# The silu and its table in program order, and TensorE's side products held behind the scan that precedes them

## The chip, the cores and the metric

The kernel runs on one core of a Trainium2 chip. The metric is the device time of one execution in microseconds (us), the median of several runs; lower is better. One execution was also recorded by the hardware profiler, and all durations below come from that record.

## What is computed

A batch of 16 images, 192 channels of 32 x 32, goes through four residual layers. Layers 0, 1 and 3 hold a recurrence along the 1024 pixels of an image; layer 2 is a depthwise convolution. The reference of layer 3, which matters most here, is in essence:

```python
xz = einsum('bchw,cd->bdhw', x, W_in) + b_in           # x: group-normed image
x_in, z = xz[:, :384], xz[:, 384:]
xc = silu(depthwise_conv4x4(x_in))                      # 384 channels
xs = [xc by rows, xc by columns, both reversed]         # 4 directions k
dt, Bm, Cm = projections of xs[k]; dt = softplus(dt)
h = h * exp(dt * A) + (dt * u) * B                      # per pixel, 16 states
y = sum(h * C)                                          # per pixel
y = layernorm(sum of the 4 directions) * silu(z)
g_out = y @ W_out + b_out
l_out = relu(bn(depthwise_conv3x3(x))) @ pw
out = w0 * g_out + w1 * l_out + x                       # w: softmax router
```

Layer 1 is of the same kind with one direction, a 4-tap convolution, two layer norms and a gate `silu(z)`.

## The kernel before

Three blocks of code run one after the other: `layer0`, `layer12` (layers 1 and 2) and `layer3`. Layers 1 and 3 are built around the same scan.

**The scan.** `scan_run` (L864) goes through units of 512 pixels and in each through the 16 states; one pair of unit and state is a step. Layer 1 has 2 units an image, so 32 steps, layer 3 has 4 directions of 2 units, so 128 steps. The 384 channels lie in three blocks t of 128 partitions. In a step

- `decay` (L904) makes exp(dt * A) on ScalarE (tile `da`, one instruction for each t, an `Exp`), for the step after this one;
- `times_b` (L882) makes u * B on ScalarE (tile `xbt`, three instructions; a fourth quarter is made on TensorE through `diag`, which GpSimd makes in `diagonals`), two steps ahead, and starts the DMA of one row of C to all partitions (tile `cb`);
- `turn` (L911) transposes xbt to the channel layout on TensorE (tile `xb`, four products for each t), one step ahead;
- `scan` (L925) is VectorE's recurrence instruction (tile `h`, L933), one for each t;
- `times_c` (L935) multiplies h by C on GpSimd (L940), after copying the last column to `carry` (L939);
- `total` (L942) transposes and adds h into `y` on TensorE (twelve products), two steps later.

`da` has five buffers, `xb` three, `h` four, `xbt` two.

**The side work.** All else of layers 1, 2 and 3 is written as Python generators that `Side` (L201) advances between the parts of a step (`side.tick`), each between a start and an end step. In layer 3, for image b, these are `prep` for the next unit (`scan_prep`, L827: softplus as an `Exp` at L841 and an `Ln` at L842 for each t, then transposes), `columns` and `tail` for the image before, `front`, `local`, `z` and `xc` for the image after.

**The tail.** `layer3_tail` (L1567) runs at steps 8 to 36 of the next image. For each half of an image it loads z (tile `tmp`, one buffer, L1574), does a layer norm (a `Square` at L361, an `Ln` at L363, an `Exp` at L364), calls `self.silu(sz)` on the loaded z, scales (L1579), multiplies on GpSimd (L1583), and later projects (L1591).

**What sets the order.** The text gives a program; a scheduler then places each engine's instructions, and may move one ahead of or behind others of its engine where no data forbids it. Every engine executes its own list in the order placed. Two things bind the scheduler by hand: `tc.keep_in_program_order(...)` on an instruction, and `tc.add_manual_dep` with class `NoSync`, which orders two instructions and adds no semaphore. In `scan_run`, `in_order` (L874) chains the transposes and totals of the scan to one another in this second way; TensorE's other products ("side products") are not bound to the chain.

**Activation tables.** ScalarE's functions lie in table sets. `Silu` needs one set, `Exp` and `Ln` are together in the set called `natural_log_exp_and_others` (`LNEXP` in the text). A load (ACT_TABLE_LOAD in the profile, LoadActFuncSet in the built program) puts a set in place. The text asks for one only in `silu` (L1204), which runs the activation and then preloads `LNEXP`; only the preload is kept in program order. Any other load is put in where the placed order needs it, at the activation that needs it.

Of the kernel before, what the change touches and what calls it, by code (L numbers as in the profile page):

```python
# [19 lines left out]
HP = 96  # L20
# [212 lines left out]


class Chunk:

# [15 lines left out]
class Program:  # L252
    def __init__(self, tc, ins, out, at):
        self.tc, self.nc, self.ins, self.out = tc, tc.nc, ins, out
        self.at96, self.at128, self.atc, self.atc0 = at
        self.nb = ins["x"].shape[0]


# [62 lines left out]
    def group_norm(self, pool, psum, x):  # L321

        nc = self.nc
        st = pool.tile([HP, 2, 2, 6], F32, name="gnst")
        mv = pool.tile([HP, 2, 2], F32, name="gnmv")
        for m in range(2):
            for i, h in enumerate(halves()):
                nc.vector.bn_stats(st[:, m, i], x[:, m, h])
            nc.vector.bn_aggr(mv[:, m], st[:, m].rearrange("p a b -> p (a b)"))
            yield 1  # L330
        ps = psum.tile([128, 512], F32, name="mm")
        nc.tensor.matmul(ps[:HP, :2], self.k("group", HP), mv[:, :, 0], start=True, stop=True)
        mean = pool.tile([HP, 2], F32, name="gnmean")
        nc.vector.tensor_copy(mean, ps[:HP, :2])
        d = pool.tile([HP, 2], F32, name="gnd")
        nc.vector.tensor_tensor(d, mv[:, :, 0], mean, SUB)
        q = pool.tile([HP, 2], F32, name="gnq")
        nc.vector.tensor_tensor(q, d, d, MUL)
        nc.vector.tensor_tensor(q, q, mv[:, :, 1], ADD)
        yield 1  # L340
        ps = psum.tile([128, 512], F32, name="mm")
        nc.tensor.matmul(ps[:HP, :2], self.k("group", HP), q, start=True, stop=True)
        r = pool.tile([HP, 2], F32, name="gnr")
        nc.vector.tensor_scalar(r, ps[:HP, :2], EPS, None, ADD)
        self.pow_mhalf(r)
        yield 1
        return mean, r, d

    def layer_norm(self, pool, psum, xs, outs, ones, p, n):

        nc = self.nc
        mean = psum.tile([128, 512], F32, name="mm")
        for i, x in enumerate(xs):
            nc.tensor.matmul(mean[:p, :n], ones, x, start=i == 0, stop=i == len(xs) - 1)
        for x, o in zip(xs, outs):
            nc.vector.tensor_tensor(o, x, mean[:p, :n], SUB)
        yield len(xs)
        var = psum.tile([128, 512], F32, name="mm")
        for i, o in enumerate(outs):
            sq = pool.tile([128, 512], F32, name="lnsq", bufs=1)  # L360
            nc.scalar.activation(sq[:p, :n], o, AF.Square)  # L361
            nc.tensor.matmul(var[:p, :n], ones, sq[:p, :n], start=i == 0, stop=i == len(xs) - 1)
        nc.scalar.activation(var[:p, :n], var[:p, :n], AF.Ln, bias=self.k("eps", p))  # L363
        nc.scalar.activation(var[:p, :n], var[:p, :n], AF.Exp, scale=-0.5)  # L364
        for o in outs:
            nc.vector.tensor_tensor(o, o, var[:p, :n], MUL)
        yield len(xs)
# [433 lines left out]
    def scan_rows(self, seen, w_x, n, bp, dp, psum):  # L801

        nc = self.nc
        ident = self.k("ident")
        m = w_x[0].shape[1]
        ps = psum.tile([128, 512], F32, name="mm")
        for t in range(3):
            nc.tensor.matmul(ps[:m], w_x[t], seen[:, t], start=t == 0, stop=t == 2)  # L810
        dbl = bp.tile([m, 512], F32, name="dbl", bufs=n)
        nc.scalar.activation(dbl, ps[:m], AF.Identity, bias=self.k("ones_row", m))
        row = dp.tile([n, NS, 512], F32, name="row", bufs=5)
        for q in range(n):
            nc.sync.dma_start(row[q], dbl[64 * q + RK + NS : 64 * q + XD])
        yield 2.6
        ps = psum.tile([128, 4, 128], F32, name="mm")
        for c in range(4):
            nc.tensor.transpose(ps[:, c, :m], dbl[:, c * 128 : (c + 1) * 128], ident[:m, :m])
        bt = bp.tile([128, 4, n, NS], F32, name="bt", bufs=4)  # L820
        nc.vector.tensor_copy(
            bt, ps.rearrange("p c (q r) -> p c q r", r=64)[:, :, :n, RK : RK + NS]
        )
        yield 0.5
        return dbl, row, bt

    def scan_prep(self, u, rows, q, xc, xt, new, w_dt, bp, psum):  # L827
# [9 lines left out]
        for t in range(3):  # L837
            ps = psum.tile([128, 512], F32, name="mm")
            nc.tensor.matmul(ps, w_dt[:, t * 128 : (t + 1) * 128], dbl, start=True, stop=True)  # L839
            e = bp.tile([128, 512], F32, name="lnsq", bufs=1)  # L840
# [6 lines left out]
        for j in range(3):  # L847
            o = slice(j * 512, (j + 1) * 512)
            if new:
                rows = xc[:, :, 512 * u.half : 512 * u.half + 512]  # L850
                ps = psum.tile([128, 512], F32, name="mm")
                for i in range(4):
                    c, t = divmod(4 * j + i, 3)
                    nc.tensor.transpose(ps[:, i * 128 : (i + 1) * 128], rows[:, t, c * 128 : (c + 1) * 128], ident)
                nc.scalar.copy(xflat[:, o], ps)
            ps = psum.tile([128, 512], F32, name="mm")
            for i in range(4):
                c, t = divmod(4 * j + i, 3)
                nc.tensor.transpose(ps[:, i * 128 : (i + 1) * 128], u.dt[:, t, c * 128 : (c + 1) * 128], ident)
            nc.vector.tensor_tensor(flat[:, o], xflat[:, o], ps, MUL)  # L860
# [3 lines left out]
    def scan_run(self, units, side, bp, psum):  # L864
# [6 lines left out]
        xbt, xb, da, h = {}, {}, {}, {}  # L871
        last = []

        def in_order(ins):  # L874

            if last:
                self.tc.add_manual_dep(
                    ins.ins, last.pop(), mybir.DependencyInfo(mybir.DependencyClass.NoSync, mybir.DependencyReason.DATA)
                )
            last.append(ins.ins.name)  # L880

# [96 lines left out]
        for i in range(len(steps) - 2, len(steps)):  # L978
            for t in range(3):
                total(i, t)  # L980
        side.close()

    def untranspose(self, y, t, psum):

        ps = psum.tile([128, 512], F32, name="mm")
        for c in range(4):
            self.nc.tensor.transpose(
                ps[:, c * 128 : (c + 1) * 128], y[:, c, t * 128 : (t + 1) * 128], self.k("ident")
# [99 lines left out]
    def depthwise(self, ps, blocks, reps, side):  # L1088

        width = W + side - 1  # L1090
        for r in range(side):
            for g, rep in enumerate(reps):
                seen = rep[:, : (15 + side) * width].rearrange("p (a b) -> p a b", b=width)[:, r : r + 16, :W]
                self.nc.tensor.matmul(  # L1094
                    ps[32 * g : 32 * g + 32], blocks[:, g * side + r], seen,
# [4 lines left out]
    def fold_norm(self, wp, psum, w, m_tiles, bias_in, bias, wname, bname, name):  # L1100
# [5 lines left out]
        for i in range(m_tiles):  # L1106
            for m in range(2):
                nc.tensor.matmul(
                    ps[:p, i : i + 1], w[:, m, i * p : (i + 1) * p], self.v96(bname, m), start=m == 0, stop=m == 1
# [35 lines left out]
    def layer1_front(self, b, sp, bp, psum):  # L1145
# [26 lines left out]
        for t in range(3):  # L1172
            for h in halves():
                ps = psum.tile([128, 512], F32, name="mm")
                for m in range(2):
                    nc.tensor.matmul(
                        ps, self.w_in[:, m, t * 128 : (t + 1) * 128], xn[:, m, h], start=m == 0, stop=m == 1
# [7 lines left out]
    def layer1_conv(self, b, bp, psum):  # L1185
# [3 lines left out]
        for t in range(3):  # L1189
            for h in halves():  # L1190
# [3 lines left out]
                for g, rep in enumerate(reps):  # L1194
                    nc.tensor.matmul(
                        ps[32 * g : 32 * g + 32], self.t_conv[:, 4 * t + g], rep[:, :512],
# [7 lines left out]
    def silu(self, x):  # L1204

        self.nc.scalar.activation(x, x, AF.Silu)
        self.tc.keep_in_program_order(self.nc.scalar.preload_act_table_set(LNEXP))

    def layer1_gate(self, b, bp, psum):
# [6 lines left out]
        for t in range(3):  # L1216
            for h in halves():
                ps = psum.tile([128, 512], F32, name="mm")
                for m in range(2):
                    nc.tensor.matmul(  # L1220
                        ps, self.w_in[:, m, DI + t * 128 : DI + (t + 1) * 128], xn[:, m, h], start=m == 0, stop=m == 1
# [6 lines left out]
    def layer1_out(self, b, bp, psum):  # L1228
# [6 lines left out]
        for h in halves():  # L1235
            for m in range(2):
                ps = psum.tile([128, 512], F32, name="mm")
                for t in range(3):
                    nc.tensor.matmul(
                        ps[:HP], self.w_out[:, t, m * HP : (m + 1) * HP], sz[:, t, h], start=t == 0, stop=t == 2  # L1240
# [6 lines left out]
    def layer1_tail(self, b, sp, bp, dp, psum):  # L1247
# [3 lines left out]
        for h in halves():  # L1251
# [8 lines left out]
            for m in range(2):  # L1260
                ps.append(psum.tile([128, 512], F32, name="mm"))
                for k in range(2):
                    nc.tensor.matmul(
                        ps[m][:HP], self.w_proj[:, k, m * HP : (m + 1) * HP], x[:, k, h], start=k == 0, stop=k == 1
# [212 lines left out]
    def layer3_local(self, b, sp, bp, psum):  # L1477
# [10 lines left out]
        for i, h in enumerate(halves()):  # L1488
# [10 lines left out]
            for m in range(2):  # L1499
                ps = psum.tile([128, 512], F32, name="mm")  # L1500
                for k in range(2):
                    nc.tensor.matmul(  # L1502
                        ps[:HP], self.w_pw[:, k, m * HP : (m + 1) * HP], l[:, k], start=k == 0, stop=k == 1
# [6 lines left out]
    def layer3_z(self, b, bp, psum):  # L1510

        nc = self.nc
        for i in range(2):
            for t in range(3):
                ps = psum.tile([128, 512], F32, name="mm")
                for m in range(2):
                    nc.tensor.matmul(  # L1517
                        ps, self.w_in[:, m, DI + t * 128 : DI + (t + 1) * 128],
# [7 lines left out]
    def layer3_xc(self, b, bp, dp, psum):  # L1526
# [6 lines left out]
        def project(t):  # L1533
            for i in range(2):
                ps = psum.tile([128, 512], F32, name="mm")
                for m in range(2):
                    nc.tensor.matmul(
                        ps, self.w_in[:, m, t * 128 : (t + 1) * 128],
# [28 lines left out]
    def layer3_tail(self, b, bp, psum):  # L1567
# [17 lines left out]
        for m in range(2):  # L1585
            for h in halves():
# [3 lines left out]
                for t in range(3):  # L1590
                    nc.tensor.matmul(  # L1591
                        ps[:HP], self.w_out[:, t, m * HP : (m + 1) * HP], v[:, t, h], start=t == 0, stop=t == 2
# [5 lines left out]
    def router(self, sp, psum, d, r):  # L1598
# [5 lines left out]
        for m in range(2):  # L1604
            wide = sp.tile([HP, HP], F32, name="wide", bufs=1)
            nc.vector.tensor_copy(wide, xm[:, m : m + 1].to_broadcast([HP, HP]))
            nc.tensor.matmul(ps[:HP, :2], wide, self.v96("3r_w", 2 * m, 2), start=m == 0, stop=m == 1)
        e = sp.tile([HP, 2], F32, name="re")
# [25 lines left out]
```

## Time and profile before

| | us |
|---|---|
| median of three runs | 17937.86 (17929.37 to 17949.53) |
| the profiled execution | 17942.07 |
| its span on the core | 17940.3 |
| PE busy | 16197.5 (90%) |
| DVE busy | 13314.9 (74%) |
| ACT busy | 12215.5 (68%) |
| POOL busy | 11472.7 (64%) |
| layer 1 and 2's scan, us 4310 to 7880: PE / DVE / ACT / POOL busy of 3570 | 3220.93 / 2729.63 / 2467.09 / 2092.00 |
| layer 3's scan, us 8112 to 17880: PE / DVE / ACT / POOL busy of 9768 | 8991.05 / 8490.39 / 8533.28 / 7894.56 |

PE is TensorE, DVE VectorE, ACT ScalarE, POOL GpSimd, SP the engine that issues most DMAs. The profiled execution is 4.2 us above the median. Its span is cut into layers by the records of the scan instruction (L933): the first one of layer 1 starts at 4310.6 us, the first one of layer 3 at 8112.7, and the last one ends at 17879.1. In layer 3 four engines are each busy for 81 to 92% of the time, so none of the busy shares alone says what sets the pace; the pace is read stretch by stretch.

A line of the groups reads: line, engine, operation, output<-inputs, shapes, count | busy us, mean ns of one | idle time of the engine just before them, and what ended it. A line of the stretches reads: the stretch, its length, then for each engine its busy time and number of instructions, the TensorE clock granted (1 is full), the DMA share and GB/s.

### The profile page before, as it was taken

The numbers are of one execution on the slowest core, as the hardware profiler recorded it, in microseconds if no ns is written. First come the engines' busy times: TensorE is split into PE (matmuls) and PEld (weight loads), VectorE is DVE, ScalarE is ACT, GpSimd is POOL, SyncE is SP. The second block draws the span as 40 slices with busy tenths as digits, with TensorE's granted clock in tenths as the row PEclk, the third lists the DMA queues.
The fourth block names the chain that finished last, engine by engine and source line by source line (L and its number), as shares of the span: only waits on it lengthen the run. The fifth ranks groups of instructions, "written<-read, shape, count | busy, mean of one in ns | idle before, by whom it ended". The sixth has DMA issues, their size and how long they took to land.

```text
span 17940.3 us, 264092 instructions
## 1 busy us (share of the span) xinstructions
PE 16197.5 (90%) x99836; PEld 11281.1 (63%) x99836; DVE 13314.9 (74%) x14875; ACT 12215.5 (68%) x19906; POOL 11472.7 (64%) x5556
## 2 busy tenths in 40 slices
PE   8999889898999999979899999999988999999998
PEld 4444444444655555546777777777777777777777
DVE  4444445444777777758888888888888888888888
ACT  2222222223766666647888898888888888988888
POOL 3333333333555555547787888787878877887878
PEclk8898898888999999989999999999999999999999
DMA  1111111112433333333333233333333332333232
GB/s 43 31 32 32 32 32 30 30 31 82 116 115 116 112 117 114 111 107 100 89 101 103 84 97 105 97 90 95 107 91 93 99 105 85 92 105 101 88 93 65
DMA packets 877953, 1511.12 MB, mean 84 GB/s; under 512 B 80336, under 2 KB 311197, under 8 KB 865834
## 3 DMA queue, kind: packets, MB, share of 16 engines
q1 hardware_dynamic: 876682, 1494.22, 28.6%
q8 instruction: 791, 12.96, 0.3%
q14 instruction: 480, 3.93, 0.1%
HBM read 1264.99 MB, written 228.92 MB: 83 GB/s over the span
## 4 chain that ended last, share of the span: by engine, by line
PE 27%; ACT 11%; DVE 8%; issue 4%; POOL 4%; DMA 1%; SPq 0%; POOLq 0%; DVEq 0%; ACTq 0%
PE y L951 7%; PE xb L917 6%; DVE h L933 6%; PE xb L920 4%; ACT da L909 4%; ACT xbt L889 3%; POOL h L940 3%; PE mm L1094 3%; PE mm L810 1%; PE mm L839 1%; PE mm L1517 1%; ACT L909 1%; ACT L842 1%; PE mm L1502 1%; ACT lnsq L842 1%
## 5 line engine op out<-in xcount | busy, mean ns | idle before, releaser
L940 POOL TENSOR_TENSOR h<-h,cb 128x1536 f32<-128x1536 f32 x2560 | 8880.1, 3472 | 1635.0 <-DVE h L933 1045.2
L909 ACT ACTIVATE da<-dt,neg_a 128x512 f32<-128x512 f32 x7680 | 5242.3, 714 | 1542.7 <-DVE h L933 1455.8
L933 DVE TENSOR_TENSOR_SCAN h<-da,carry,xb 128x512 f32<-128x512 f32 x3840 | 4664.9, 1262 | 812.8 <-PE xb L920 605.4
L951 PE MATMUL y<-const,h 128*128 128x128 f32 x30720 | 4739.7, 277 | 132.9 <-DVE ysum L1391 54.6
L933 DVE TENSOR_TENSOR_SCAN h<-da,xb 128x512 f32<-128x512 f32 x3840 | 4439.2, 1202 | 389.9 <-PE xb L920 255.2
L917 PE MATMUL xb<-const,xbt 128*128 128x128 f32 x23040 | 4128.4, 283 | 490.1 <-ACT xbt L889 266.7
L889 ACT ACTIVATE xbt<-ut,bt 128x384 f32<-128x384 f32 x7680 | 4172.9, 603 | 227.5 <-PE xb L917 225.0
L917 PEld LDWEIGHTS xb<-const,xbt 128*128 128x128 f32 x23040 | 2776.7, 143 | 1940.3 <-ACT xbt L889 678.8
L951 PEld LDWEIGHTS y<-const,h 128*128 128x128 f32 x30720 | 3705.2, 144 | 322.9 <-issue 258.8
L920 PE MATMUL xb<-diag,ut 128*128 128x128 f32 x15360 | 3028.5, 279 | 0.0
L920 PEld LDWEIGHTS xb<-diag,ut 128*128 128x128 f32 x15360 | 2400.0, 197 | 68.2 <-issue 68.2
L458 PE MATMUL conv<-ypad,w_conv 96*96 96x512 f32 x2304 | 1253.8, 665 | 3.1 <-ACT y L465 3.1
L899 POOL TENSOR_TENSOR diag<-const,bt 128x512 f32<-128x512 f32 x640 | 668.3, 1044 | 584.7 <-PE xb L920 363.7
L939 POOL COPY carry<-h 128x3 f32<-128x3 f32 x1280 | 255.0, 199 | 1152.2 <-DVE h L933 887.1
L753 POOL TENSOR_TENSOR hs<-h,mhm 128x384 f32<-128x384 f32 x128 | 106.4, 831 | 1027.9 <-DVE den L758 902.0
L636 POOL TENSOR_TENSOR e<-e,const 128x1536 f32<-128x1536 f32 x128 | 444.8, 3475 | 437.3 <-DMA e<-row 406.4
L458 PEld LDWEIGHTS conv<-ypad,w_conv 96*96 96x96 f32 x2304 | 380.4, 180 | 450.1 <-issue 431.1
L839 PE MATMUL mm<-dbl,w_dt 45*128 45x512 f32 x960 | 551.2, 659 | 27.0 <-DVE v L1413 16.1
L638 ACT ACTIVATE e<-e 128x1536 f32<-128x1536 f32 x128 | 189.6, 1482 | 453.9 <-POOL e L637 408.0
L706 PEld LDWEIGHTS num<-v,p 128*128 128x128 f32 x3072 | 433.1, 218 | 78.2 <-issue 55.3
L843 DVE SCALAR_TENSOR_TENSOR dt<-lnsq,mm 128x512 f32<-128x512 f32 x480 | 322.4, 672 | 211.2 <-ACT lnsq L842 210.7
L1094 PE MATMUL mm<-rep,taps 128*32 128x512 f32 x3072 | 428.6, 614 | 27.3 <-DMA rep<-xr 21.4
(272 smaller groups left out, 18026.7 us busy)
## 6 DMA issues: line engine op xcount, KB each, us to landing
cb<-row SPq DMA_DIRECT2D x2560, 256.0 KB
rep<-xr SPq DMA_DIRECT2D x384, 331.0 KB
e<-row SPq DMA_DIRECT2D x128, 768.0 KB
rep<-xin SPq DMA_DIRECT2D x384, 256.0 KB
rep<-xr SPq DMA_DIRECT2D x384, 228.8 KB
x<-x SPq DMA_DIRECT2D x48, 768.0 KB
xr<-xin SPq DMA_DIRECT2D x48, 612.5 KB
xr<-xpad SPq DMA_DIRECT2D x32, 867.0 KB
```

The lines of the kernel that those rows point to most:

```text
L458: nc.tensor.matmul(ps[:HP], self.w_c2[:, k, t, m * HP : (m + 1) * HP], yp[:, k, r0 : r0 + 16, t % 3 : t % 3 + W], start=t + k == 0, stop=t ...
L636: nc.gpsimd.tensor_tensor(e, e, self.k0("mask")[:, None, :].to_broadcast([128, NH, 128]), ADD)
L839: nc.tensor.matmul(ps, w_dt[:, t * 128 : (t + 1) * 128], dbl, start=True, stop=True)
L889: nc.scalar.activation(t[:, c], u.ut[:, c], AF.Copy, scale=u.bt[:, c, n : n + 1])
L899: nc.gpsimd.tensor_tensor(d, ident[:, None, :].to_broadcast([128, 4, 128]), u.bt[:, 3, n : n + 4][:, :, None].to_broadcast([128, 4, 128]), ...
L909: nc.scalar.activation(da[i, t], u.dt[:, t], AF.Exp, scale=u.neg_a(t, n))
L917: in_order(nc.tensor.transpose(xb[i, t][:, c * 128 : (c + 1) * 128], xbt[i][:, c, t * 128 : (t + 1) * 128], ident))
L920: in_order(nc.tensor.matmul(xb[i, t][:, 384:], u.ut[:, 3, t * 128 : (t + 1) * 128], u.diag[n // 4][:, n % 4], start=True, stop=True, skip_ ...
L933: nc.vector.tensor_tensor_scan(hv, dv, xv, 0.0 if first else u.carry_in[:, n, t : t + 1], MUL, ADD)
L940: nc.gpsimd.tensor_tensor(h[i], h[i], u.c.pop(n)[:, None, :].to_broadcast([128, 3, 512]), MUL)
L951: in_order(nc.tensor.matmul(u.y[:, j], h[i][:, t, c * 128 : (c + 1) * 128], ident, is_transpose=True, start=n == 0 and j % 4 == 0, stop=n ...
L1094: self.nc.tensor.matmul(ps[32 * g : 32 * g + 32], blocks[:, g * side + r], seen, start=r == 0, stop=r == side - 1, skip_group_check=True,)
```

## The change

Two edits. The silu activation itself is kept in program order too, as the preload after it already was. And every product of TensorE outside layer 0's own goes through a small object, `Matrix`, which adds the same kind of order-only dependency to it: behind the last chained instruction of the scan that precedes it in the text. The chain itself stays: `in_order` sets the dependency through the same object. Outside `scan_run` (`after` is None) nothing is added. No computation, tile, buffer, DMA or semaphore of the program text is changed.

```diff
+class Matrix:
+    def __init__(self, tc):
+        self.tc, self.tensor, self.after = tc, tc.nc.tensor, None
+
+    def behind(self, ins):
+        if self.after is not None:
+            why = mybir.DependencyInfo(mybir.DependencyClass.NoSync, mybir.DependencyReason.DATA)
+            self.tc.add_manual_dep(ins.ins, self.after, why)
+        return ins
+
+    def matmul(self, *args, **kw):
+        return self.behind(self.tensor.matmul(*args, **kw))
+
+    def transpose(self, *args, **kw):
+        return self.behind(self.tensor.transpose(*args, **kw))
...
+        self.pe = Matrix(tc)
...
-            nc.tensor.matmul(ps, w_dt[:, t * 128 : (t + 1) * 128], dbl, start=True, stop=True)
+            self.pe.matmul(ps, w_dt[:, t * 128 : (t + 1) * 128], dbl, start=True, stop=True)
...
-        last = []
+        self.pe.after = None
 
         def in_order(ins):
 
-            if last:
-                self.tc.add_manual_dep(
-                    ins.ins, last.pop(), mybir.DependencyInfo(mybir.DependencyClass.NoSync, mybir.DependencyReason.DATA)
-                )
-            last.append(ins.ins.name)
+            self.pe.behind(ins)
+            self.pe.after = ins.ins.name
...
+        self.pe.after = None
         side.close()
...
     def silu(self, x):
 
-        self.nc.scalar.activation(x, x, AF.Silu)
+        self.tc.keep_in_program_order(self.nc.scalar.activation(x, x, AF.Silu))
         self.tc.keep_in_program_order(self.nc.scalar.preload_act_table_set(LNEXP))
```

The replacement of `nc.tensor.matmul` or `nc.tensor.transpose` by `self.pe.matmul` or `self.pe.transpose` is the same in `group_norm`, `layer_norm`, `scan_rows`, `scan_prep`, `untranspose`, `depthwise`, `fold_norm`, all of layer 1 and 2's side work, `layer3_local`, `layer3_z`, `layer3_xc`, `layer3_tail` and `router`.

## Prediction

> **What bounds the kernel now.** I read the page first. TensorE (PE) is busy for 90% of the span, but the chain that ended last gives it only 27% and ScalarE (ACT) 11%; two entries of that chain carry a line and no tile, so they are table loads.
>
> ```profile
> PE 27%; ACT 11%; DVE 8%; issue 4%; POOL 4%; DMA 1%; SPq 0%; POOLq 0%; DVEq 0%; ACTq 0%
> PE y L951 7%; PE xb L917 6%; DVE h L933 6%; PE xb L920 4%; ACT da L909 4%; ACT xbt L889 3%; POOL h L940 3%; PE mm L1094 3%; PE mm L810 1%; PE mm L839 1%; PE mm L1517 1%; ACT L909 1%; ACT L842 1%; PE mm L1502 1%; ACT lnsq L842 1%
> ```
>
> Next, the ACT groups within layer 3's scan (8112 to 17880 us): how many loads, and in front of what.
>
> ```profile
> L909 ACT ACT_TABLE_LOAD x127 | 162.9, 1283 | 2.3
> L842 ACT ACT_TABLE_LOAD x96 | 123.2, 1283 | 1.7
> L1206 ACT ACT_TABLE_LOAD x46 | 59.0, 1283 | 58.9 <-DMA tmp<-sz 58.3
> L1207 ACT ACT_TABLE_LOAD x46 | 59.0, 1283 | 0.8
> L841 ACT ACT_TABLE_LOAD x15 | 19.2, 1283 | 0.3
> L363 ACT ACT_TABLE_LOAD x15 | 19.2, 1283 | 0.3
> ```
>
> Only the 46 at L1206 and 46 at L1207 belong to a silu. The other 253 (127 + 96 + 15 + 15) are swaps between Exp and Ln, after a silu has run and before the preload of the set that holds both; in layers 1 and 2 the groups show none. The ACT timeline of one such stretch (image 3, steps 18 to 20) shows the mechanism:
>
> ```profile
> 10038.41 1.32 ACT L909 ACTIVATE da<-dt,neg_a 128x512 f32<-128x512 f32 x2
> 10043.60 1.28 ACT L1206 ACT_TABLE_LOAD   x1 [3.87 <-DMA tmp<-sz]
> 10044.89 1.49 ACT L1206 ACTIVATE tmp<-tmp 128x1536 f32<-128x1536 f32 x1
> 10046.40 1.28 ACT L909 ACT_TABLE_LOAD   x1
> ...
> 10053.00 1.28 ACT L842 ACT_TABLE_LOAD   x1
> 10054.29 0.72 ACT L842 ACTIVATE lnsq<-lnsq,const 128x512 f32<-128x512 f32 x1
> 10055.03 1.28 ACT L909 ACT_TABLE_LOAD   x1
> ```
>
> The reader is to see two things: silu stands at the head of ACT's list and waits 3.87 us for its z, and from then on each Ln costs two loads, until the preload at 10085.98.
>
> Last, equal stretches side by side (columns: length, then PE, PEld, DVE, ACT, POOL busy, then granted clock): steps 16 to 23 of image 0 and of image 5, then steps 32 to 47 and 80 to 95 of image 15, then 80 to 95 and 96 to 109 of image 5.
>
> ```profile
> 8192.90:8231.90 39.00, 38.95 (x285) 28.80 (x284) 33.70 (x33) 35.64 (x61) 31.50 (x13) 1.00 0.30 79
> 11262.00:11318.40 56.40, 44.77 (x245) 34.10 (x244) 37.67 (x38) 51.21 (x73) 36.80 (x15) 0.85 0.18 57
> 17489.90:17559.40 69.50, 63.33 (x461) 54.02 (x460) 58.97 (x55) 69.31 (x115) 59.75 (x35) 0.95 0.29 85
> 17696.90:17758.10 61.20, 57.70 (x455) 49.70 (x453) 60.02 (x55) 60.16 (x106) 59.99 (x22) 1.00 0.25 71
> 11581.20:11658.80 77.60, 73.54 (x539) 55.41 (x541) 63.04 (x56) 73.32 (x119) 59.86 (x22) 0.98 0.41 127
> 11658.80:11729.00 70.20, 69.89 (x575) 52.16 (x568) 61.15 (x59) 62.20 (x102) 61.72 (x35) 1.00 0.41 135
> ```
>
> The ACT groups inside them count the loads: none, 11, 7 swaps, none, 7 (six swaps and a preload), and the 2 of silu(xc). Image 15's pair is nearly a measurement of a swap by itself, since both hold 16 steps and one unit's preparation: 8.3 us for 7 loads, 1.19 us each against 1.283 us long. So ACT has almost no slack to hide them. In image 5's steps 16 to 23 ACT is busy 51.2 us and waits 3.9 for z: together 55.1 of 56.4.
>
> [...] In the trace three xb transposes take 0.49 us, and about 0.85 after PE idled 3.5 us at 10046.8 to 10050.3; the granted clock of the 56.4 us stretch is 0.85. So an ACT stall is paid again, in part, on PE.
>
> **The change, part by part.** *Silu in program order.* The order of the built programs' instructions has 480 loads in the whole program before and 227 after: 253 fewer, all in layer 3. Every silu now stands directly before its preload. Counted in `da` and `xbt` instructions ahead of it (ACT's list runs some two and a half steps ahead of the scan), the first half's silu of the tail moves from step 77 of the image before to 15.8, the second's from 18.8 to 23.8; the z transfers move by one step at most. Nothing is added. The sum for an image with a tail in it:
>
> 1. Steps 16 to 23: 9 loads fewer (11 swaps and silu loads become 2), 11.5 us of ACT, and 3.9 us of waiting for z, since its transfer is issued one step later and its silu comes five steps later, some 20 us of room against the 4.08 us that the chain shows for the transfer. That leaves ACT 39.7 us, PE 44.8 x 0.85 = 38 at full clock, DVE 37.7, POOL 36.8. Four engines at 37 to 40 do not overlap perfectly; image 0 needs 39.0. I take 42.5: gain 14 (11 to 16).
> 2. Steps 80 to 95: 7 loads go, 9.0 us of ACT. What is late next is PE: 73.5 of 77.6 us busy, with the convolution of the next image. I take 4.5 of the 9.0 (2 to 7).
> 3. Silu of the first half: its two loads and 1.49 us, 4.05 in all, leave steps 75 to 76, where ACT is busy 32.3 of 34.4 us (gain 1, 0 to 2), and arrive in steps 13 and 14, where ACT is busy 11.1 of 12 us, just before its own stretch (cost 3, 1 to 4).
>
> Sum 14 + 4.5 + 1 - 3 = 16.5 us, for images 1 to 14: 231. Image 0 has only items 2 and the first of 3: 5.5. Image 15 has items 1 and 3 (11), and no next image, so its own first silu runs at step 32 already, and with it come 15 loads between steps 24 and 65, which go behind the last scan: 15 x 1.19 = 18; together 29. Total 265 (180 to 350).
>
> As a check from the other side: adding up the pieces of the chain of waits in layer 3, 230 of the swaps (294 us) and 62 us of the transfer `tmp<-sz` lie on it. 356 is what could go if nothing else came late; 265 is three quarters.
>
> *Side products behind the scan.* No instruction and no semaphore is added. In the placed order layer 0 is unchanged; in layer 1 the side products of steps 12 to 21 stand 0.1 to 0.6 steps later, in layer 3 the projections of the last preparation of an image move from step 110.5 to 113.8 and their transposes from 113.7 to 118.2, the rest by less than about a step on average. Behind a side product that waits stand the scan's transposes, and behind these VectorE. PE's idle time before side products in layer 1's scan is some 230 us, but the largest part keeps its place (72 us before the group norm's product L332). I take layer 1 as no change, from -60 to +60 us. In layer 3, `dbl` (L812) waits 97.5 us for L810 in 48 of the 63 preparations, 2.0 us each; the last one of an image, 15 in all, never waits now and has a gap as short as the others afterwards: up to 15 x 2 = 30 us lost in steps where DVE is the fuller engine (62.0 of 63.8 us). Against it, products pulled up no more before PE's scan work (L1591 idles 40 us, L362 34, L839 22) may give back as much. I take 0 for the sum, -30 to +30.
>
> The profiled execution took 17942 us; 17942 - 265 = 17677. The median lies 4 us lower, so 17675.
>
> **The rivals.** *A: nearly all of it comes.* ACT's loads and the wait go one to one, and PE stays at full clock: 356 plus some 20 for the clock, 17942 - 370 = 17572. For it: image 15's 93%. Against it: PE's 94% in steps 80 to 95.
> *B: PE or the mixture takes the place of ACT.* Steps 16 to 23 shrink only to 48, steps 80 to 95 by 2: 8.5 + 2 + 1 - 3 = 8.5 an image, 119, with image 0 and 15 another 20: 17942 - 140 = 17802. For it: four engines within 10% of each other. Against it: image 0's 39.0 us.
> *C: slower, through TensorE's order.* A side product can no longer pass a chained scan product that waits for its data, so PE idles where it had filled the gap. In layer 1 PE is idle 349 us of 3570 (22 an image). To eat 265 us the idle time there would have to rise by three quarters; if it doubled, 17942 - 265 + 349 = 18026. The point from which it decides is 300 us, some 19 us an image. Against it: the shifts are half a step.
> *D: the change doesn't do what it says.* Excluded for the loads by the built order; for the second edit it is the case of my forecast, a change of 0.
>
> **How the numbers follow.** My forecast 0.60 (its own range 17590 to 17760), A 0.12, B 0.20, C 0.05, a still smaller gain 0.03. A measurement of this kernel tells about 0.2% (36 us) from no change. Faster by more: forecast, A and B and a part of the last, 0.94; same 0.03; slower 0.03, most of C. The range from 17560 to 17805 takes in A and B nearly to their middles.
>
> **What would show it.** Loads 227 in all, none at L841, L842, L363 or L909 (their lines moved on) within layer 3. Steps 16 to 23 of a middle image at 41 to 45 us, no wait for `tmp<-sz` before silu, clock near 1.00 there. Steps 80 to 95 at 71 to 75 us with PE full. Layer 3's scan 9500 instead of 9766 us, layer 1's within 60 of 3569. I am wrong if layer 1 changes by more than that, if steps 16 to 23 stay over 48, or if the preparation at steps 110 to 126 delays the next image's first step.

## The result: slower, and the profile after

The changed kernel takes 18070.83 us in the median (18060.65 to 18101.16), the kernel before 17943.6 in the same comparison: a ratio of 1.0075, 95% interval 1.0057 to 1.0092. 17675 was forecast.

The first edit did what it says. The ACT groups within layer 3's scan (8188 to 17994 us of the changed kernel's trace) hold no load that isn't a silu's (L1225) or its preload's (L1226), and nothing waits for z any more:

```profile
L1225 ACT ACT_TABLE_LOAD x45 | 57.7, 1283 | 0.8
L1226 ACT ACT_TABLE_LOAD x45 | 57.7, 1283 | 0.6
```

Yet layer 3's scan went from 9766 to 9804 us and layer 1's from 3563.5 to 3653.5 (all lengths of layer 1 in this document run from the first scan instruction to the start of the last step; to its end it is 5 us more). The chain of work that ended last, from the page after, shows what took ACT's place:

```profile
PE 31%; DVE 10%; ACT 9%; issue 3%; POOL 2%; DMA 1%; SPq 0%; DVEq 0%; POOLq 0%; ACTq 0%
PE mm L249 10%; PE y L969 8%; DVE h L951 7%; PE xb L935 7%; PE xb L938 4%; ACT da L927 3%; ACT xbt L907 3%; POOL h L958 2%; PE mm L252 1%; DVE ysum L1410 1%; ACT ysum L1408 0%; ACT lnsq L863 0%; ACT L1226 0%; ACT L1225 0%; ACT lnsq L862 0%
```

PE went from 27% to 31%. All side products share one line now, L249 (transposes L252), since they go through `Matrix`. `ysum`, the copy or sum of a finished y out of PSUM, stands among these entries now; on the whole chain it went from 101 us to 176. The row of the y products in the page's groups, before and then after:

```profile
L951 PE MATMUL y<-const,h 128*128 128x128 f32 x30720 | 4739.7, 277 | 132.9 <-DVE ysum L1391 54.6
```

```profile
L969 PE MATMUL y<-const,h 128*128 128x128 f32 x30720 | 4781.7, 279 | 325.5 <-DVE ysum L1410 168.6
```

The last columns are PE's idle time just before these products, and what ended most of it: 192.6 us more, 174.5 of it for `ysum`. `y` has one buffer of 1536 columns. The first y product of a new unit (state 0) must wait until the copy or the sum of the last unit's y has read that buffer. The PE timeline of image 5 at step 82 to 83 shows what stands around this product, before and then after (columns: start, length, engine, line, product, count, idle time before it):

```profile
11590.88 0.39 PE L920 MATMUL xb<-diag,ut 128*128 128x128 f32 x2
11591.20 1.12 PE L839 MATMUL mm<-dbl,w_dt 45*128 45x512 f32 x2
11592.25 1.13 PE L1537 MATMUL mm<-xpad,w_in 96*128 96x512 f32 x2
11593.22 0.60 PE L951 MATMUL y<-const,h 128*128 128x128 f32 x4
```

```profile
11689.67 0.39 PE L938 MATMUL xb<-diag,ut 128*128 128x128 f32 x2
11692.70 0.78 PE L969 MATMUL y<-const,h 128*128 128x128 f32 x4 [2.65 <-ACT ysum L1408]
11693.42 2.07 PE L249 MATMUL mm<-dbl,w_dt 45*128 45x512 f32 x2
11695.42 0.90 PE L935 MATMUL xb<-const,xbt 128*128 128x128 f32 x3
```

Before, two side products (two records each) stood ahead of the waiting y product and filled its wait: no idle time is shown before it. After, the same product from `dbl` stands behind it: PE idles 2.65 us, then does the side work all the same, and takes 2.07 us instead of 1.12 for it, at a lowered clock (0.79 in these two steps, below). The scan's next xb comes after all that. In these 2.65 us the trace has no product and no weight load of PE either (PEld idles 2.81 us there): nothing passes the waiting product.

Each unit has such a place. The mean length of equal stretches over images 2 to 13, from the starts of the scan instruction in the traces (the last three columns are experiments, below), in us:

| steps | before | after | e1 silu alone | e5 first y binds | e3 free at first y |
|---|---|---|---|---|---|
| 16 to 23 | 57.19 | 45.27 | 40.95 | 42.13 | 43.16 |
| 24 to 31 | 36.29 | 41.19 | 38.57 | 39.08 | 41.30 |
| 40 to 47 | 42.42 | 44.06 | 47.85 | 43.93 | 44.06 |
| 48 to 55 | 36.73 | 39.57 | 37.15 | 40.24 | 37.08 |
| 64 to 71 | 42.96 | 45.38 | 43.00 | 45.30 | 42.96 |
| 80 to 87 | 43.13 | 42.92 | 37.66 | 42.41 | 38.23 |
| 112 to 119 | 30.36 | 34.83 | 30.81 | 35.20 | 31.37 |

Steps 16 to 23 fell by 12 us, within the forecast's 11 to 16. The stretches that grew by 2.4 to 4.5 us (from step 48 on) each hold the start of a unit, and most of their growth lies in one step of each: 51, 67 and 115. At 80 to 87 the same loss ate the silu's gain of 5.5 us.

### The profile page after: what moved, and what is told of

Same layout as the page of the kernel before. It is cut to its first block, busy times and chain, and to the rows that moved or that the text cites. A ratio compares the mean times of both kernels' runs of the same rounds, so it can differ in the third digit from the quotient of the medians.

```text
span 18058.9 us, 263706 instructions
## 1 busy us (share of the span) xinstructions
PE 16270.8 (90%) x99836; PEld 11368.8 (63%) x99836; DVE 13344.6 (74%) x14875; ACT 11919.8 (66%) x19653; POOL 11461.9 (63%) x5556
## 4 chain that ended last, share of the span: by engine, by line
PE 31%; DVE 10%; ACT 9%; issue 3%; POOL 2%; DMA 1%; SPq 0%; DVEq 0%; POOLq 0%; ACTq 0%
PE mm L249 10%; PE y L969 8%; DVE h L951 7%; PE xb L935 7%; PE xb L938 4%; ACT da L927 3%; ACT xbt L907 3%; POOL h L958 2%; PE mm L252 1%; DVE ysum L1410 1%; ACT ysum L1408 0%; ACT lnsq L863 0%; ACT L1226 0%; ACT L1225 0%; ACT lnsq L862 0%
## 5 line engine op out<-in xcount | busy, mean ns | idle before, releaser
L969 PE MATMUL y<-const,h 128*128 128x128 f32 x30720 | 4781.7, 279 | 325.5 <-DVE ysum L1410 168.6
L935 PE MATMUL xb<-const,xbt 128*128 128x128 f32 x23040 | 4061.6, 283 | 379.5 <-DVE h L951 233.7
L249 PE MATMUL mm<-dbl,w_dt 45*128 45x512 f32 x960 | 556.0, 661 | 34.4 <-DVE v L1432 16.1
L249 PE MATMUL mm<-rep,t_dw 96*32 96x512 f32 x2304 | 430.9, 610 | 24.1 <-DMA rep<-xr 17.9
```

Source lines behind the costliest of these rows:

```text
L249: return self.behind(self.tensor.matmul(*args, **kw))
L935: in_order(nc.tensor.transpose(xb[i, t][:, c * 128 : (c + 1) * 128], xbt[i][:, c, t * 128 : (t + 1) * 128], ident))
L969: in_order(nc.tensor.matmul(u.y[:, j], h[i][:, t, c * 128 : (c + 1) * 128], ident, is_transpose=True, start=n == 0 and j % 4 == 0, stop=n ...
```

## The experiments

Theory W, the wait at the first y, against three rivals: S (the silu's new place does it), L (all side products stand later, and that starves the work behind them), and, for layer 1, the projections. e9 has a theory of its own for layer 1, P: VectorE's small sums collide with GpSimd. Where a difference in us is derived from a ratio, it is that part of 17940.

### e1 and e2: each edit alone

```diff
 e1:  before, and
-        self.nc.scalar.activation(x, x, AF.Silu)
+        self.tc.keep_in_program_order(self.nc.scalar.activation(x, x, AF.Silu))
 e2:  after, and the reverse of it
```

> Only the silu is kept in program order; TensorE's products are placed as before. Theory W (a wait at the head of PE's list: at the first y product of a unit PE waits some 2.6 us for the copy of the y before it, and the side products that used to stand ahead of it now stand behind it): the loss is all TensorE's order, so this comes near the forecast made for silu, 17680 to 17740 us (ratio 0.985 to 0.989), 227 table loads, layer 1 at 3569 us as before. Theory S (the silu's new place in steps 13 and 14 pushes the work of all that follows, and the order on TensorE is innocent): 17950 to 18070, with layer 3 as long as in the changed kernel.

> Only TensorE's side products are bound behind the scan; silu is free as before. Theory W: the whole loss and none of silu's gain, 18270 to 18340 us (ratio 1.018 to 1.022), 480 loads, layer 1 at about 3659 us as in the changed kernel. Theory S: within 0.3% of before, 17900 to 18000. If the two edits meet at the same steps (PE's waits hide behind the table loads, or the reverse), this time and the one of silu alone do not add up to the changed kernel's +127 us: a sum that is off by over 50 us would show it.

e1: 17726.4 us, ratio 0.9897 (0.9881 to 0.9912). e2: 18276.18 us, ratio 1.0202 (1.0188 to 1.0216). S is out: silu alone brings 185 us, TensorE's order alone costs 362. By the ratios the two add up to a loss of 177 where the change has 135; in the profiled spans they add up to 94.8 (17717.7 and 18257.7 against 17940.3) where it has 118.6. They add, within some 40 us, though not because the edits leave each other alone: e2's trace has 412 table loads, where I expected the 480 of before, so the order on TensorE moves ACT's list too. Layer 1 is 3560.6 in e1 and 3652.7 in e2: its loss is the order's.

### e3, e5 and e4: the first y product

e3 takes one product's role as an anchor away; e5 leaves only that; e4 leaves the order and shortens the wait.

```diff
 e3, e5:  the chain is kept apart from what side products are bound behind
+        chain = Matrix(self.tc)
-        def in_order(ins):
-            self.pe.behind(ins)
-            self.pe.after = ins.ins.name
+        def in_order(ins, anchor):
+            chain.behind(ins)
+            chain.after = ins.ins.name
+            if anchor:
+                self.pe.after = chain.after
 anchor:  e3 all but the y products with n == 0;  e5 only y with n == 0 and j == 0
 e4:
-                u.y = psum.tile([128, 12, 128], F32, name="y", bufs=1)
+                u.y[part] = psum.tile([128, 4, 128], F32, name=f"y{part}", bufs=1)
...
-                if n == NS - 1:
-                    u.finish(u.y.rearrange("p a b -> p (a b)"))
+            if n == NS - 1:
+                u.finish(u.y[part].rearrange("p a b -> p (a b)"), part)
```

> The changed kernel, but the y products of a unit's first state (n = 0) are no anchor: side products are bound behind the scan's last chained product other than these, so that they may stand ahead of the y product that waits. 12 of a unit's 384 chained products are concerned. Theory W: most of the loss at the starts of the units comes back, in layer 3 some 14 us for each image (steps 3, 51, 67, 83, 99, 115), in layer 1 some of steps 16 to 19: 17790 to 17880 us. Rival L (side products that stand later all along, half a step each, starve the chain of preparations and VectorE, and the y wait is only where it shows): 18030 to 18090, as the changed kernel.

> The kernel with silu alone, and of the second edit only this: side products are bound behind the first y product of the unit that precedes them in the text (one product of each unit's 384), behind nothing else. It is the reverse of e3. Theory W: that single product makes layer 3's whole loss; layer 1's products are placed as before, so layer 1 stays at 3560 to 3570 us, layer 3's scan is 9780 to 9860 (silu alone 9562), 17960 to 18030 us in all. Rival L (the many small shifts): near silu alone, 17720 to 17790.

> The changed kernel, with y made as three tiles of 512 columns (one buffer each, the same room in all) and copied out in three pieces, each as soon as its own last product is in. The order rule on TensorE is untouched. Theory W: the first y product of a unit then waits only for a piece that was finished a third of a step's products earlier and takes a third of the time to copy, so the 2.6 us at the head of PE's list goes to below 1 us: 17750 to 17880 us; against it stand two more copies for each of 160 units with their fixed cost[...]. Rival L: 18030 to 18130, no better than the changed kernel.

e3: 17775.53 us, 0.992 (0.9907 to 0.9932). e5: 17982.37 us, 1.0022 (1.0016 to 1.0029). e4: 17663.9 us, 0.9863 (0.9849 to 0.9876). e4 came out faster than the range written down for it, e3 at the lower edge of its own. In layer 3 the scan takes 9562 us in e1 and 9815.5 in e5: one product of a unit's 384 as an anchor costs 253 us, as much as was lost there in all. (This is a net figure: in steps 40 to 47 of the table e5 is 3.9 us an image shorter than e1.) Without these anchors it is 9516.5 (e3), although every other side product is bound. So L is out for layer 3. In the sum the many small shifts cost nothing there; in the table they lose 2.2 and 2.7 us an image at steps 16 to 31 (e3 against e1) and win 3.8 at steps 40 to 47. The group of y products in e5, and in e4:

```profile
L972 PE MATMUL y<-const,h 128*128 128x128 f32 x30720 | 4738.8, 277 | 323.9 <-DVE ysum L1413 167.9
```

```profile
L971 PE MATMUL y<-const,h 128*128 128x128 f32 x30720 | 4740.9, 277 | 17.9 <-POOL h L958 17.7
```

e5 has the idle time of the changed kernel (325.5). With y in three pieces it is 17.9, less than the 132.9 of before, with TensorE's order rule as in the change. The price is small: three copies of 568 ns on ACT in place of one of 1417. The same two steps (82 and 83 of image 5) in stretches, of before, after, e5, e1 and e4 (length, then PE, PEld, DVE, ACT, POOL busy, granted clock, DMA share and GB/s):

```profile
11588.59:11600.61 12.02, 10.92 (x61) 7.13 (x61) 8.01 (x8) 11.96 (x18) 9.92 (x5) 1.00 0.71 215
```

```profile
11687.81:11703.88 16.07, 13.42 (x61) 8.62 (x60) 7.90 (x8) 12.37 (x21) 10.53 (x5) 0.79 0.52 177
```

```profile
11605.24:11621.20 15.96, 13.32 (x61) 8.77 (x60) 7.91 (x8) 12.36 (x21) 10.56 (x5) 0.79 0.54 178
```

```profile
11498.13:11508.91 10.78, 10.24 (x61) 7.01 (x60) 7.83 (x9) 10.78 (x19) 10.58 (x5) 1.00 0.51 171
```

```profile
11529.10:11539.60 10.50, 10.24 (x61) 7.04 (x60) 7.82 (x8) 10.50 (x21) 10.50 (x5) 1.00 0.51 166
```

PE has the same products, 61 records, in all five. The 16 us of the change and of e5 are the wait and the clock of 0.79; ACT at 11.96 of 12.02 was the limit before. The gain at this place was there (12.02 us became 10.78 in e1), and four times as much was lost again (16.07).

e3 had one miss: I expected part of layer 1's loss back. Layer 1 is 3653.5 in it, as in the changed kernel; its loss is another.

### e6 and e9: layer 1

In layer 1 the traces put most of the loss into steps 16 to 19 of an image (mean of images 2 to 13: 39.31 us before, 46.51 after), and nearly all of it, 93 us over the 16 images, into steps 12 to 21. The placed order of TensorE around the front's norms is, for image 6 (X for xb products, y for y products, each with their number; in brackets the side products; the figure ahead is the step):

```
before  12  X1 y4 X4 y4 [mm<-xt]2 X4 y4 X3
        13  X1 y4 X4 y4 [mm<-gnmv]1 X4 y4 X3
        14  X1 [mm<-gnq]1 y4 X4 y4 X4 y4 X1 [mm<-xf]2 [mm<-lnsq]1 X2
after   12  X1 y4 X4 y4 X4 y4 X3
        13  X1 y4 [mm<-xt]2 X4 y4 [mm<-gnmv]1 X4 y4 X3
        14  X1 y4 X4 y3 [mm<-gnq]1 y1 X4 y4 X3
        15  X1 y4 X4 y4 X1 [mm<-xf]2 [mm<-lnsq]1 X3 y3 [mm<-lnsq]1 y1 X3
```

The layer norm's first product (`mm<-xt`), the group norm's second (`mm<-gnq`) and the norm's products from `xf` behind it each go back by 0.3 to 0.7 of a step. e6 frees the layer norm's products alone; e9 leaves the order and takes the group norm's square off VectorE.

```diff
 e6:  in layer_norm
-            self.pe.matmul(mean[:p, :n], ones, x, ...)
+            nc.tensor.matmul(mean[:p, :n], ones, x, ...)
-            self.pe.matmul(var[:p, :n], ones, sq[:p, :n], ...)
+            nc.tensor.matmul(var[:p, :n], ones, sq[:p, :n], ...)
 e9:  in group_norm
-        nc.vector.tensor_tensor(q, d, d, MUL)
-        nc.vector.tensor_tensor(q, q, mv[:, :, 1], ADD)
+        nc.scalar.activation(ps[:HP, 2:4], d, AF.Square)
+        nc.vector.tensor_tensor(q, mv[:, :, 1], ps[:HP, 2:4], ADD)
```

> The changed kernel, but the products of the layer norm are not bound. Layer 1's loss (3563.5 to 3653.5 us in the profiles, still there in e2 to e4) must come from something other than the first y. Theory N: a layer norm's first product (mm from xt, in front of the group norm) goes from step 12 to 13 of an image, and the group norm and all that hangs on it go back by about a step with it; freed, layer 1's products lie as before, so layer 1 comes back to 3560 to 3575 us while layer 3 stays near 9800: 17960 to 18000 us in all. Rival: what hurts in layer 1 is the projections and transposes at steps 16 to 19, bound as before: 18050 to 18090, layer 1 at 3640 to 3660.

> The changed kernel, but the group norm's d*d is a Square on ScalarE into PSUM instead of a product of two SBUF operands on VectorE, and the sum with var reads it there; the value is the same and TensorE's order stays nearly as in the changed kernel. In the changed kernel's trace that product (L359) takes 2.68 us instead of 0.16 in 36 of its 47 places in layers 1 and 3, since GpSimd's multiplication runs, and PE waits 3.8 us for the sum behind it. Theory P (this collision is the core of layer 1's loss of 90 us): layer 1 at 3585 to 3625 us and the whole at 17985 to 18040. Rival N' (the norm's chain is simply a step later, the collision is hidden by it): layer 1 at 3640 to 3655, 18050 to 18085 in all.

e6: 17962.22 us, 1.0007 (0.9999 to 1.0015). Layer 1 is 3566.3, layer 3 9786.5. With the layer norm's products freed, all of layer 1's loss is gone; that the projections stay bound does nothing. e9: 18001.12 us, 1.0052 (1.0039 to 1.0065), layer 1 at 3607.9: 46 of the 90 us, as P asked for. The collision that P means stands in the changed kernel's timelines of VectorE, GpSimd and PE, at steps 14 and 15 of image 6:

```profile
5741.52 0.13 DVE L357 TENSOR_TENSOR gnd<-gnmv,gnmean 96x2 f32<-96x2 f32 x1
5741.58 1.21 DVE L951 TENSOR_TENSOR_SCAN h<-da,xb 128x512 f32<-128x512 f32 x1
5742.71 2.68 DVE L359 TENSOR_TENSOR gnq<-gnd 96x2 f32<-96x2 f32 x1
```

```profile
5741.94 3.44 POOL L958 TENSOR_TENSOR h<-h,cb 128x1536 f32<-128x1536 f32 x1
```

```profile
5746.62 0.48 PE L249 MATMUL mm<-gnq,const 96*96 96x2 f32 x2 [3.81 <-DVE gnq L360]
```

The square of 96 x 2 numbers takes 2.68 us: it starts while GpSimd multiplies and ends 0.01 us after it, at 5745.39. The scan instruction behind it waits, and PE, with `gnq`'s product at its head, waits 3.81 us. By the same count over layers 1 and 3, the square started during such a multiplication in 22 of 47 places before and in 36 after. All 14 more are this norm, the one of layer 1's front: none of its 15 squares before, 14 after. Layer 1's other group norm, at steps 22 to 24, has 14 of 15 in both kernels.

Yet P's number came out by luck. e9 takes both collisions away, and of its 46 us, 28 come from steps 22 to 24, where the change had lost 2.5. Of the 93 us lost at steps 12 to 21 it gives back 8: it wins 44 us at step 15 and loses 49 at step 16. PE's idle time in layer 1 before `gnq`'s products falls from 70.0 us to 16.6, and before the products from `xf`, next in the norm, it rises from 12.5 to 53.8. VectorE's groups of layer 1, change and e9, show what `xf` waits for:

```profile
L1182 DVE TENSOR_SCALAR xf<-x,gnmean,gnr 96x1024 f32<-96x1024 f32 x30 | 23.7, 830 | 7.5 <-POOL gnr L307 7.4
L1182 DVE TENSOR_SCALAR xf<-x,gnmean,gnr 96x1024 f32<-96x1024 f32 x30 | 23.7, 829 | 40.0 <-POOL gnr L307 40.0
```

`gnr` is a step of the norm on GpSimd; in e9 it waits at image 6 behind GpSimd's next multiplication. So the collision is new in the change, but it is not shown to cost layer 1 anything by itself. Layer 1's loss comes from the later place of the layer norm's products (e6); which of the waits at steps 12 to 21 carries it stays open.

### e7, e8 and e10: a version that beats both

```diff
 e7:  e1 and e4's y in three tiles
 e8:  e7, and in group_norm
-        nc.vector.tensor_tensor(d, mv[:, :, 0], mean, SUB)
+        nc.vector.tensor_tensor(d, mv[:, :, 0], ps[:HP, :2], SUB)
+        nc.vector.tensor_tensor(ps[:HP, 2:4], mv[:, :, 0], ps[:HP, :2], SUB)
-        nc.vector.tensor_tensor(q, d, d, MUL)
-        nc.vector.tensor_tensor(q, q, mv[:, :, 1], ADD)
+        nc.vector.tensor_tensor(ps[:HP, 4:6], d, ps[:HP, 2:4], MUL)
+        nc.vector.tensor_tensor(q, mv[:, :, 1], ps[:HP, 4:6], ADD)
 e10:  e8, and in layer3_front
+                ps = psum.tile([128, 512], F32, name="mm")
-                    y2[:, h], y2[:, h], AF.Relu, ...
+                    ps[:HP], y2[:, h], AF.Relu, ...
-                nc.vector.scalar_tensor_tensor(x[:, m, h], y2[:, h], 6.0, x[:, m, h], MIN, ADD)
+                nc.vector.scalar_tensor_tensor(x[:, m, h], ps[:HP], 6.0, x[:, m, h], MIN, ADD)
```

> Silu in program order, y in three tiles and three copies, TensorE's side products free as before: the candidate that should beat both kernels. If the wait at the first y costs time in the kernel before too (54.6 us of PE's idle time in front of y were put down to the copy), and layer 1 keeps its 3560 us: 17580 to 17640. Rival: the free side products fill that wait already, so the three pieces bring nothing and cost two more copies a unit: 17710 to 17760, no better than silu alone.

> e7, and the group norm's small sums (d, d*d and d*d + var, 96 x 2 elements) take one operand from PSUM each, so that none reads two operands from SBUF; one such instruction more, the value is the same. In the silu-alone trace they take 0.13 to 0.16 us, or 2.4 to 3.3 us when GpSimd's multiplication of 128 x 1536 runs (29 of 94), until that ends. Theory P (VectorE waits for GpSimd there, and the scan behind it waits too): 30 to 80 us faster than e7, with none of these sums over 0.5 us. Rival: the next instruction with two SBUF operands (x from tmp and x) meets the same multiplication instead, or PE is late anyway: within 15 us of e7.

> e8, and the relu of layer 3's front is written to a PSUM tile (name mm) instead of back into tmp, so that x from tmp and x on VectorE reads one operand from PSUM; nothing else. That instruction takes 0.67 us alone and 1.7 in the median, 3.5 at most, in 58 of its 64 places in e8. Theory P: some 58 us of VectorE's time at steps 37 to 41 go, the fuller engine there: 20 to 60 us faster than e8, 17530 to 17575. Rival: the two mm buffers are held by ScalarE and VectorE now, side products of TensorE wait for them: 17580 to 17640.

e7: 17653.95 us, 0.9837 (0.9824 to 0.985), between the two values written down; against e1 it gains 54 us on layer 3 (9507.6 against 9562) and 21 on layer 1. Against e4, which has TensorE's order rule in addition, layer 1 is 75 us shorter and layer 3 49 us longer: once nothing waits at the first y, the rule costs nothing in layer 3. e8: 17592.13 us, 0.9804 (0.9791 to 0.9816), 62 us faster than e7. e10: 17510.09 us, 0.978 (0.9767 to 0.9794), some 43 us faster than e8 by the ratios. The tile views of e7 and e10 show the disputed instructions (after the count: shortest, median and longest in ns):

```profile
L338 DVE TENSOR_TENSOR gnq<-gnd x64: 128/157/3368, 36.3 to 16669.7; 96x2 f32<-96x2 f32 x64
L339 DVE TENSOR_TENSOR gnq<-gnq,gnmv x64: 126/157/3320, 36.5 to 16669.9; 96x2 f32<-96x2 f32 x64
```

```profile
L1471 DVE SCALAR_TENSOR_TENSOR x<-mm,x x64: 658/661/687, 7917.5 to 16528.6; 96x512 f32<-96x512 f32 x64
```

In e8 the sum q (L340 there) takes 154 ns at most; in e10 the front's sum takes 687 at most, where it took 3473 with both operands in SBUF (e8). Since TensorE's order rule seemed to gain in layer 3 in e4 (49 us against e7), e11 adds it to e10 for layer 3 alone:

```diff
 e11:  e10, in scan_run
+        chain = self.pe if self.bind else Matrix(self.tc)
 with bind False in layer12 and True in layer3, and the chain's products ordered through it
```

> e10, with TensorE's side products bound behind the scan in layer 3 alone, by the rule of the change (layer 1 is placed as in e10). In e4 and e7, which differ in this rule, layer 3's scan took 9458.9 and 9507.6 us: with no wait at the first y the rule even seemed to gain 49 us. If it does so by itself: 9365 to 9390 us for layer 3 (e10 9421.5), 17450 to 17485 in all. Rival: the 49 us were the collisions with GpSimd at steps 32 to 47, which e10 has removed in another way: layer 3 at 9410 to 9470, 17500 to 17560, no better than e10.

e11: 17521.16 us, 0.9771 (0.9758 to 0.9785), no different from e10. Layer 3 is 27 us shorter (9394 against 9421.5), between the two ranges written down, and layer 1 12.5 longer although its products are placed as in e10, so a difference of this size can't be told in one trace. e10 and e11 are the fastest kernels of this study, some 395 and 410 us below the one before, by the ratios.

## Why the prediction was wrong

*Side products behind the scan* is the step that failed. I took 0 for its sum, -30 to +30 us for layer 3 and -60 to +60 for layer 1. It costs 253 us in layer 3 by e5 against e1, and 90 us in layer 1. The sum priced the waits of side products, and what stands behind them; the wait of a chained product, with the side products now behind it, it put at nothing, since they move by half a step on average. What counted in layer 3 was which waiting product they were moved behind; for layer 1 the runs show only that it is the layer norm's later products. That layer 1 moved by more than 60 us was one of the prediction's own signs of being wrong. The 242 us by which layer 3 is longer in the change than in e1, the 90 of layer 1 and the 61 that the silu brought less than forecast (below) make 393 of the 396 us between forecast and result. The view that would have told it was there before: PE's 132.9 us of idle time before y, and the timeline with a side product between the last xb and the first y of a unit. In the placed order of before, six of an image's eight units have one to five side products just ahead of that y; after, none has. The other two, the first and second, are those where little was lost (0.5 us at step 3, none at step 19).

Rival C had the mechanism word for word, with a chance of 0.05, but put it into layer 1 and asked for a doubling of all its idle time there. The place was the first y of each unit in layer 3; the price 16 us an image (601.9 to 617.9 in e1 and e5, mean of images 1 to 14).

*Loads.* 90 within layer 3's scan, where 345 were, and 227 in all; right.

*Item 1, steps 16 to 23:* 14 forecast, 16.2 in e1, 11.9 in the change.

*Item 2, steps 80 to 95:* 4.5 forecast, 5.3 in e1 (77.66 to 72.40), 0.5 in the change (77.15), since the first y at step 83 took it. PE was late next, as said, but by waiting, not by being full.

*Item 3:* cost 3 at steps 8 to 15, 2.4 measured; gain 1 at steps 72 to 79, 1.9 measured. Image 15 gave 29.8 us in e1, where 29 was forecast.

*The silu's sum*, 265 us (180 to 350), was 204 in layer 3 of e1: within its range, but 11.8 us an image (images 1 to 14) in place of 16.5. The missing term is at steps 24 to 47, which I had left alone: steps 40 to 47 grew by 5.4 us an image and steps 24 to 31 by 2.3. The DVE and the POOL timeline of e1 there, image 5:

```profile
11293.69 3.48 DVE L1464 SCALAR_TENSOR_TENSOR x<-tmp,x 96x512 f32<-96x512 f32 x1
...
11304.49 3.32 DVE L339 TENSOR_TENSOR gnq<-gnq,gnmv 96x2 f32<-96x2 f32 x1
```

```profile
11293.16 3.46 POOL L940 TENSOR_TENSOR h<-h,cb 128x1536 f32<-128x1536 f32 x1
...
11304.34 3.46 POOL L940 TENSOR_TENSOR h<-h,cb 128x1536 f32<-128x1536 f32 x1
```

With the loads gone, the front's work runs at other moments, and VectorE's sum there, with two SBUF operands, starts during GpSimd's multiplication in 57 of 64 places instead of 18; its busy time went from 61.9 us to 99.7. The group norm's three small sums take about as long as before (53.1 us in layer 3 before, 51.5 in e1), another of them being hit. e8 and e10 took both kinds away, and steps 40 to 47 went from 47.62 us in e7 to 44.39 and 41.52. So these collisions lie on the path there, and the front's sum, whose remedy is worth 2.9 us an image there in e10, is the part that had grown. Why the moments shifted, and what made steps 24 to 31 longer, is not shown.

## What to carry to other kernels

When an order rule is added between two lists of one engine, look for the few instructions in the first list that wait for a buffer, and see what stood ahead of each: here a mean shift told nothing. An accumulator with one buffer can be split into pieces that are copied out one by one; that took PE's idle time before y from 325.5 us to 17.9 with no more room (e4), and made the order rule harmless in layer 3. A rule that binds filler work should anchor it to products whose data is early, not to one that waits for another engine (253 us in layer 3 for one such anchor, e5). And when an experiment returns the number that a theory asked for, look whether it came from the place that the theory names (e9).

## What the hardware showed beside that

The group norm's sums of two SBUF operands, 96 x 2 numbers each, take 0.13 to 0.16 us alone in the changed kernel. Its squares in layers 1 and 3 that start while a GpSimd multiplication of SBUF operands runs, 36 of 47, take 2.26 to 3.37 us, and each ends 0.01 to 0.02 us after that multiplication. With one operand in PSUM the sum q takes 0.154 us at most (e8), though 29 of its 47 in layers 1 and 3 start during a multiplication.

The waits of PE cost more than their length here. In the change's step 83, the products after 2.65 us of idle time, less than the 3.5 us of the prediction's example, took 2.07 us instead of 1.12, and the granted clock of the two steps was 0.79 instead of 1.00. The wait and the lower clock stand together here; what lowers the clock is not shown. Over layer 3's scan PE is busy 9010 us in e5 and 8887 in e1, with the same products and a granted clock of 0.96 instead of 0.98: 123 of the 253 us that this one anchor cost are slower products, and the rest is idle time.
